# Causal attention layer: exponentials in pieces of 1024 columns, the exponential table loaded again behind each root, and the layers of the last four tiles in batches of two, one and one

## The chip, the core and the metric

The kernel runs on one core of one Trainium2 chip. The metric is the time of one execution on the device in microseconds; a change of 0.2% is 4 us here. The core has a matrix engine (TensorE; PE in the profile, PEld its weight loads), a vector engine (VectorE, DVE), a scalar engine for functions such as the exponential and the root (ScalarE, ACT), a general engine (GpSimd, POOL), and queues that start transfers (SyncE, SP). Each engine works through its own list of instructions; semaphores order them against each other. TensorE writes its results into a small accumulator memory (PSUM) from which the other engines copy them into the working memory (SBUF).

## What is computed

The input is an image of 256 channels and 64 x 64 positions. A first layer (windowed linear attention, not touched by the change) adds to it. Then the 4096 positions become tokens of 256 numbers, and a causal attention layer with a small network follows; a routed network of two experts ends the kernel. Cut to what matters here:

```python
t = _to_tokens(x)                                   # 4096 tokens x 256
t = t + _L1_attn_ref(_ln_t(t), ...)
t = t + _L1_ffn_ref(_ln_t(t), ...)

def _L1_attn_ref(x, ...):
    q, k, v = x @ Wq.T + bq, x @ Wk.T + bk, x @ Wv.T + bv
    A = where(causal, q @ k.T, MASK_FILL) / sqrt(256)
    A = softmax(A)
    out = _layernorm(A @ v + x, g_ln, beta_ln)
    h = relu(out @ W1.T + b1) @ W2.T + b2
    return _layernorm(h, g_lnff, beta_lnff)
```

The router of the last layer takes the mean over all tokens, so no expert work can start before the causal layer is through with its last token.

## The kernel before

The causal layer (`causal_attention`, L891) works on 32 tiles of 128 tokens, all in float32. Four tiles make a group `g`. The tiles 31 down to 12 are "large" and drive the outer loop, round by round; the tiles 0 to 11 are "small", and each of the first twelve rounds takes one of them along. From round 12 on, in which tile 19 is attended, there is no small tile left.

Four functions do the work:

- `queries(g)` (L911): two groups of matmuls make the queries `qT` of four tiles; ScalarE copies them out (L918). `need` calls it once for each group.
- `scores(i)` (L939): in parts of 512 columns, PE multiplies queries by keys into the accumulator `pa` (L957), of which there are two; ScalarE copies each part into the row buffer `s` or `ss` (L959), POOL masks the diagonal, VectorE takes the maximum of each part (L965). After the last part the maxima are merged into `nb` (L968, L969) and one exponential runs over the whole row, up to 4128 columns (L970).
- `attend(i)` (L974) returns steps. Step by step PE transposes four blocks of exponentials into `pt` (L987; two buffers), VectorE copies them to `sT` (L990), and PE multiplies them with the values into `po` (L1001). The last step ends with `finish`: division, addition of the input, statistics, and the tile is noted in `done`.
- `layers(g, j0, j1)` (L1031) returns the six stages that follow the attention for the tiles j0 to j1 of a group: `first` (root of the variances, normalisation, L1041), `turn` (transposes L1049, copies `aT` L1050), `hidden` (matmuls L1058, Relu L1060), `last` (matmuls L1068, addition L1070, statistics, root, L1075 and L1076, statistics), `norm` (root, normalisation L1083; nothing for PE), `turn_again` (transposes L1091, ScalarE's copies L1092 that also sum for the router).

Three stages contain a root. `rsqrt` (L708) takes it on ScalarE (Sqrt, L709) and inverts it on VectorE (L710). ScalarE holds one table of functions at a time; where the next function needs another one, the build puts a table load ahead of it (ACT_TABLE_LOAD in the trace).

The order on PE is the order in which the program is written (`tc.manual_schedule(engines={PE})`); the build's planner chooses the order of the other engines' instructions. The stages of `layers` are put into a list `later`, and each call of `one()` takes the next stage from it. In each round the order is: scores of the small tile and `one()`; all parts but the last of the next large tile's scores, `one()`, the first transposes of this round's large tile, the last part; half of its steps, `one()`, the other half; the small tile's attention; `one()`. In the last round alone every step is followed by `one()`. Thus some 17 us lie between `last` and `turn_again` of a group in most rounds.

The last group (tiles 12 to 15, `BIG` is 12) is batched in its own way: when three of its tiles are through (15, 14, 13) their layers start together, and tile 12's layers come alone at the very end. `given.parts` counts the batches, and `sums` has a column for each.

The opening: while the first row (tile 31) is scored in eight parts, the values are computed in between. Then round 0 begins with `need(0)`, the queries of the small tiles 0 to 3.

Of the kernel before, what the change touches and what calls it, by code (L numbers as in the profile page):

```python
# [11 lines left out]
F32 = mybir.dt.float32  # L12
BF16 = mybir.dt.bfloat16
I32 = mybir.dt.int32
AF = mybir.ActivationFunctionType
# [4 lines left out]
P = 128  # L20
# [684 lines left out]
    nc.vector.bn_aggr(out=mv, in_=st)  # L705


def rsqrt(nc, var, eps):  # L708
    nc.scalar.activation(var, var, AF.Sqrt, bias=eps)  # L709
    nc.vector.reciprocal(var, var)  # L710


BIG = NT - 20
# [146 lines left out]
class Given:  # L860
# [3 lines left out]
    def __init__(self, nc, a, pool, causal):  # L864
        def tile(name, shape, src=None):
            s = pool.tile(shape, F32, name=name)
            if src is not None:
                nc.gpsimd.dma_start(out=s, in_=src)
            return s

        self.gam, self.bet = causal.row["gamma"], causal.row["beta"]
        self.b1 = tile("b1", [NE, FF], a["b1"])
        self.b2 = tile("b2", [NE, D], a["b2"])
        self.wr = tile("wr", [P, DC, NE], a["Wr"].rearrange("(p c) e -> p c e", c=DC))
        self.br = tile("br", [P, NE], a["br"].partition_broadcast(P))
        self.ei = tile("ei", [P, NE])
        nc.gpsimd.iota(self.ei, pattern=[[1, NE]], base=0, channel_multiplier=0, allow_small_or_imprecise_dtypes=True)
        self.pi = tile("pi", [P, 1])
        nc.gpsimd.iota(self.pi, pattern=[[0, 1]], base=0, channel_multiplier=1, allow_small_or_imprecise_dtypes=True)

        self.before = tile("before", [P, NE, NE])
        nc.gpsimd.memset(self.before, 1.0)
        nc.gpsimd.affine_select(out=self.before, in_=self.before, compare_op=ALU.is_gt, fill=0.0, base=0,
                                pattern=[[1, NE], [-1, NE]], channel_multiplier=0)
        self.after = tile("after", [NT, D + 1])
        self.stats = tile("stats2", [P, NT, 2])
        self.sums = tile("sums2", [P, DC, NQ + 1])
        self.parts = 0


def causal_attention(tc, t, ident, eps5, causal, big, given):  # L891
# [4 lines left out]
    with ExitStack() as ctx:  # L896
# [42 lines left out]
        def scores(i):  # L939

            n = (i + 1) * P
            large = i >= BIG
            s = sm.tile([P, N + NT if large else BIG * P + NT], F32, name="s" if large else "ss")
            ss[i] = s
            g, starts = i // 4, list(reversed(range(0, n, 512)))
            nbs = sm.tile([P, 10], F32, name="nbs")

            nc.gpsimd.memset(s[:, n : n + NT], -3e38)  # L948
            if i < NT - 1:
                nc.gpsimd.memset(s[:, n + i : n + i + 1], MASK_FILL)  # L950

            def part(at):
                b = starts[at]
                m = min(512, n - b)
                pp = ps.tile([P, 512], F32, name="pa")
                for c in range(DC):
                    nc.tensor.matmul(pp[:, 0:m], lhsT=qTs[g][:, c, i * P - g * 512 : n - g * 512],  # L957
                                     rhs=x[b // 512][c][:, 0:m], start=(c == 0), stop=(c == DC - 1))
                nc.scalar.activation(s[:, b : b + m], pp[:, 0:m], AF.Identity, bias=v[i][:, D + 1 : D + 2])  # L959
                if at == 0:  # L960
                    diag = s[:, i * P : n]
                    nc.gpsimd.affine_select(out=diag, in_=diag, compare_op=ALU.is_ge, fill=MASK_FILL,
                                            base=0, pattern=[[-1, P]], channel_multiplier=1)
                    m += NT
                nc.vector.tensor_reduce(nbs[:, at : at + 1], s[:, b : b + m], AX.X, ALU.max)  # L965
                if at == len(starts) - 1:
                    nb = sm.tile([P, 1], F32, name="nb")
                    nc.vector.tensor_reduce(nb, nbs[:, 0 : len(starts)], AX.X, ALU.max)  # L968
                    nc.vector.tensor_scalar_mul(nb, nb, -1.0 / 16.0)  # L969
                    nc.scalar.activation(s[:, 0 : n + NT], s[:, 0 : n + NT], AF.Exp, bias=nb, scale=1.0 / 16.0)  # L970

            return [lambda at=at: part(at) for at in range(len(starts))]

        def attend(i):  # L974

            n = (i + 1) * P
            s = ss[i]
            cols = [(j * P, P) for j in range(i + 1)] + [(n, NT)]
            groups = [cols[at : at + 4] for at in range(0, len(cols), 4)]
            g = i // 4  # L980
            state = {}

            def turn(at):
                pt = ps.tile([P, 512], F32, name="pt")
                sT = sm.tile([P, 512], F32, name="sT", bufs=3)
                for j, (b, m) in enumerate(groups[at]):
                    nc.tensor.transpose(pt[0:m, j * P : (j + 1) * P], s[:, b : b + m], ident)  # L987
                full = P * sum(m == P for _, m in groups[at])
                if full:
                    nc.vector.tensor_copy(sT[:, 0:full], pt[:, 0:full])  # L990
                if full < P * len(groups[at]):
                    nc.vector.tensor_copy(sT[0:NT, full : full + P], pt[0:NT, full : full + P])
                state[at] = sT

            def add(at):
                if at == 0:
                    state["acc"] = ps.tile([P, 512], F32, name="po")
                acc, sT = state["acc"][:, 0 : D + 1], state.pop(at)
                for j, (b, m) in enumerate(groups[at]):
                    rhs = v[b // P][:, 0 : D + 1] if m == P else after  # L1000
                    nc.tensor.matmul(acc, lhsT=sT[0:m, j * P : (j + 1) * P], rhs=rhs, start=(b == 0), stop=(m != P))  # L1001
                if at == len(groups) - 1:
                    finish(acc)

            def finish(acc):
                if g not in atts:
                    atts[g] = (sm.tile([P, 4, D], F32, name="att", bufs=3), sm.tile([P, 4, 2], F32, name="mvs", bufs=3), [])
                att, mvs, done = atts[g]
                xn = normalised(nc, sm, t[:, i, :], stats[:, i, 0:1], stats[:, i, 1:2], "xn", 2)
                l = sm.tile([P, 1], F32, name="l")  # L1010
                nc.vector.reciprocal(l, acc[:, 0:1])
                aj = att[:, i - 4 * g, :]
                nc.vector.scalar_tensor_tensor(aj, acc[:, 1:], l, xn, op0=ALU.mult, op1=ALU.add)
                statistics(nc, sm, aj, mvs[:, i - 4 * g, :])
                done.append(i)
                if 4 * g != BIG:
                    if len(done) == 4:
                        later.extend(layers(g, 0, 4))
                elif len(done) == 3:
                    later.extend(layers(g, 1, 4))  # L1020
                elif len(done) == 4:
                    later.extend(layers(g, 0, 1))

            def step(at):
                if at + 1 < len(groups):
                    turn(at + 1)
                add(at)

            return [lambda: turn(0)] + [lambda at=at: step(at) for at in range(len(groups))]

        def layers(g, j0, j1):  # L1031
# [3 lines left out]
            state = {}  # L1035

            def first():
                rsqrt(nc, mvs[:, j0:j1, 1], eps5)
                for j in js:
                    aj = att[:, j, :]  # L1040
                    nc.vector.tensor_scalar(aj, aj, mvs[:, j, 0:1], mvs[:, j, 1:2], op0=ALU.subtract, op1=ALU.mult)  # L1041
                    nc.gpsimd.tensor_add(t[:, 4 * g + j, :], t[:, 4 * g + j, :], row["beta_lnff"])
# [19 lines left out]
            def last():  # L1062
                y, hT = att, state["hT"]
                mvy = sm.tile([P, 4, 2], F32, name="mvy")
                for j in js:
# [3 lines left out]
                                         start=(c == 0), stop=(c == DC - 1))  # L1069
                    nc.vector.tensor_add(y[:, j, :], py[:, 0:D], row["b2"])  # L1070
                    statistics(nc, sm, y[:, j, :], mvy[:, j, :])
                rsqrt(nc, mvy[:, j0:j1, 1], eps5)
                for j in js:
                    yj, tj = y[:, j, :], t[:, 4 * g + j, :]
                    nc.vector.scalar_tensor_tensor(yj, yj, mvy[:, j, 0:1], row["g_lnff"], op0=ALU.subtract, op1=ALU.mult)  # L1075
# [1 line left out]
                    statistics(nc, sm, tj, given.stats[:, 4 * g + j, :])  # L1077

            def norm():
                rsqrt(nc, given.stats[:, 4 * g + j0 : 4 * g + j1, 1], eps5)  # L1080
                for j in js:
                    s = given.stats[:, 4 * g + j, :]
                    nc.vector.tensor_scalar(att[:, j, :].rearrange("p (c q) -> p c q", c=DC),  # L1083
# [15 lines left out]
        with tc.manual_schedule(engines={mybir.EngineType.PE}):  # L1099
# [16 lines left out]
            for at, part in enumerate(scores(larges[0])):  # L1116
                part()
                if at < 3:
                    causal.values(6 - at, value_psum)
                if at == 4:  # L1120
                    behind()
            for r, i in enumerate(larges):
                small = smalls.pop(0) if smalls else None
                if small is not None:
# [5 lines left out]
                if r + 1 < len(larges):  # L1130
# [4 lines left out]
                    one()  # L1135
                    todo.pop(0)()
                    parts[-1]()
                if r == len(larges) - 1:
                    while todo:
                        todo.pop(0)()  # L1140
                        one()
# [189 lines left out]
```

## Time and profile before

| | us |
|---|---|
| median of 3 runs | 1993.42 (1993.35 to 1994.79) |
| the profiled execution, its own time | 1994.53 |
| its span, first to last instruction | 1992.8 |
| window layer, until the causal stage (about) | 0 to 1018 |
| first causal matmuls to the end of tile 20's round | 1018 to 1552 |
| rounds of tiles 19 to 13 | 1552.25 to 1713.5 |
| tile 12 and the last layers | 1713.5 to 1748.5 |
| router | 1748.5 to 1762 |
| experts | 1762 to 1993 |

The stages of the causal layer by window: in the rounds of tiles 19 to 13 PE is busy 152.19 of 161.25 us at full clock, DVE 87.47 and ACT 57.75. In the 35 us from 1713.5 to 1748.5 PE is busy 24.32 us, and the mean granted clock is 0.78. There are 32 exponentials of scores with 12 table loads ahead of them (L970), each load 1283 ns.

How to read the lines below: in the page's first part, busy time, share of the span and number of instructions; in the chain, shares of the span by engine. A line of waits has who waited for whom, the total in us, how often, and the longest. A line of the timeline has the start, the duration, the engine, the line of the kernel, the operation, what it writes and reads with shapes, the number of instructions merged, and in brackets the idle time of the engine before it and what ended it.

### The profile page before, as it was taken

How to read it: one execution, taken by the hardware profiler on the slowest of the kernel's cores; microseconds unless marked ns; L12 is line 12 of the kernel's file. 1: busy time of each engine (PE TensorE's matmuls, PEld its weight loads, DVE VectorE, ACT ScalarE, POOL GpSimd, SP SyncE). 2: the span in 40 equal slices, each digit the busy share in tenths (PEclk: the TensorE clock that was granted, in tenths of full speed). 3: DMA queues.
4: the chain of work that ended last, by engine and by line, in shares of the span. 5: the costliest groups of instructions: out<-in, count | busy, mean ns of one | idle time of the engine just before them, and what ended most of it. 6: DMA issues, size and time to landing. Idle time of an engine off the chain costs nothing.

```text
span 1992.8 us, 46271 instructions
## 1 busy us (share of the span) xinstructions
PE 1859.6 (93%) x20326; PEld 1218.4 (61%) x20326; DVE 1000.5 (50%) x2190; ACT 777.4 (39%) x1331; POOL 431.8 (22%) x709
## 2 busy tenths in 40 slices
PE   4999999999999999999999999999999999879998
PEld 2655565555665555555575656665666666657777
DVE  4644555544554565555663444554553655443343
ACT  1566444444456644444414233233333234223322
POOL 1384323232155123333110000000000000031220
PEclk9999999999999999999999999999999999879999
DMA  7211100000331100000100000000000000010000
GB/s 242 82 52 45 29 13 18 13 18 12 104 92 40 45 18 18 13 13 13 50 2 0 1 0 1 0 1 0 1 0 1 0 1 0 1 43 22 21 22 22
DMA packets 66890, 53.34 MB, mean 27 GB/s; under 512 B 37568, under 2 KB 56792, under 8 KB 66688
## 3 DMA queue, kind: packets, MB, share of 16 engines
q1 hardware_dynamic: 57296, 31.87, 5.8%
q10 hardware_dynamic: 8128, 14.67, 2.1%
q0 software_dynamic: 1264, 3.84, 0.6%
q8 instruction: 159, 2.61, 0.6%
q14 instruction: 43, 0.35, 0.1%
HBM read 32.93 MB, written 17.44 MB: 25 GB/s over the span
## 4 chain that ended last, share of the span: by engine, by line
PE 42%; DVE 6%; ACT 3%; issue 1%; POOL 0%; ACTq 0%; DVEq 0%; POOLq 0%
PE po L1001 11%; PE pa L957 10%; PE ph L1265 6%; PE py L1285 6%; PE pt L987 2%; PE pm L1058 1%; PE acc L391 1%; PE pm L1068 1%; DVE lnst L704 1%; PE ps L505 1%; DVE sT L990 1%; PE ps L358 1%; DVE nbs L965 1%; PE pm L916 1%; ACT s L970 1%
## 5 line engine op out<-in xcount | busy, mean ns | idle before, releaser
L327 ACT ACTIVATE pm<-ps 128x512 f32<-128x512 f32 (+19 forms) x734 | 362.4, 558 | 348.4 <-issue 194.1
L329 DVE TENSOR_SCALAR pm<-ps 128x512 f32<-128x512 f32 (+23 forms) x442 | 267.6, 636 | 315.7 <-PE ps L358 234.5
L391 PE MATMUL acc<-pm,vh 128*32 128x248 f32 (+22 forms) x3424 | 218.5, 356 | 16.8 <-DVE pm L329 16.7
L358 PE MATMUL ps<-q,kh 32*128 32x248 f32 (+23 forms) x3424 | 204.8, 354 | 0.0
L957 PE MATMUL pa<-k,qT 128*128 128x512 f32 (+3 forms) x416 | 180.2, 574 | 7.1 <-ACT qT L918 5.6
L349 PE MATMUL ps<-table,table 32*128 32x192 bf16 (+19 forms) x2512 | 143.1, 261 | 24.4 <-ACT rn L477 8.4
L990 DVE COPY sT<-pt 128x512 f32<-128x512 f32 (+3 forms) x144 | 92.7, 644 | 142.9 <-PE pt L987 142.7
L391 PEld LDWEIGHTS acc<-pm,vh 128*32 128x32 f32 x3424 | 87.3, 110 | 108.5 <-issue 60.8
L349 PEld LDWEIGHTS <-table 32*128 32x128 bf16 x2512 | 50.0, 92 | 162.5 <-issue 155.7
L358 PEld LDWEIGHTS ps<-q,kh 32*128 32x128 f32 x3424 | 142.6, 188 | 7.3 <-issue 2.5
L426 POOL TENSOR_TENSOR y<-y,rn 128x512 f32<-128x512 f32 x32 | 41.3, 1290 | 449.5 <-DVE y L425 297.9
L959 ACT ACTIVATE s<-pa,v 128x512 f32<-128x512 f32 (+3 forms) x112 | 73.8, 661 | 152.1 <-PE pa L957 151.9
L957 PEld LDWEIGHTS pa<-k,qT 128*128 128x128 f32 x416 | 75.7, 191 | 89.3 <-issue 72.4
L965 DVE TENSOR_REDUCE nbs<-s 128x1 f32<-128x512 f32 (+4 forms) x120 | 77.6, 652 | 80.4 <-ACT s L959 59.1
L1285 PE MATMUL py<-w,hT 128*128 128x256 f32 x512 | 111.8, 379 | 0.0
L1001 PE MATMUL po<-kh,sT 128*128 128x257 f32 x406 | 102.8, 395 | 8.7 <-DVE sT L990 8.5
L1285 PEld LDWEIGHTS py<-w,hT 128*128 128x128 f32 x512 | 97.3, 190 | 15.7 <-issue 1.9
L391 PE MATMUL acc<-pm,v 128*32 128x192 f32 (+11 forms) x1600 | 98.5, 360 | 3.9 <-DVE pm L329 2.4
L358 PE MATMUL ps<-q,k 32*128 32x192 f32 (+11 forms) x1600 | 98.4, 359 | 0.0
L1001 PEld LDWEIGHTS po<-kh,sT 128*128 128x128 f32 x406 | 74.7, 195 | 22.4 <-DVE sT L990 13.2
L505 PE MATMUL ps<-l0wo,y 128*128 128x256 f32 x384 | 87.0, 383 | 0.0
L948 POOL MEMSET s<- 128x32 f32 x20 | 2.5, 124 | 376.4 <-PE pt L987 348.4
(304 smaller groups left out, 2899.0 us busy)
## 6 DMA issues: line engine op xcount, KB each, us to landing
oscratch<-ov ACTq DMA_DIRECT2D x32, 256.0 KB
ov<-oscratch SPq DMA_DIRECT2D x32, 256.0 KB
t<-in_xT SPq DMA_DIRECT2D x32, 128.0 KB
vscratch<-v SPq DMA_DIRECT2D x32, 128.0 KB
vh<-vscratch SPq DMA_DIRECT2D x16, 256.0 KB
raw<-in_x SPq DMA_DIRECT2D x7, 512.0 KB
raw<-in_x ACTq DMA_DIRECT2D x7, 512.0 KB
out<-y SPq DMA_DIRECT2D x7, 512.0 KB
```

The costliest lines, as they stand in the source:

```text
L327: nc.scalar.activation(dst, src, AF.Relu)
L329: nc.vector.tensor_scalar_max(dst, src, 0.0)
L349: nc.tensor.matmul(got[h][:, spot].rearrange("p (y x) -> p y x", y=part.r1 - part.r0), lhsT=spread[hs, int(part.vertical), :], rhs=bias[hs ...
L358: nc.tensor.matmul(got[h][:, spot].rearrange("p (y x) -> p y x", y=part.r1 - part.r0), lhsT=keys[hs], rhs=q[hs, part.r0 : part.r1, part.c0 ...
L391: nc.tensor.matmul(out, lhsT=v, rhs=pm[:, h, spot].rearrange("p (y x) -> p y x", y=part.r1 - part.r0), start=fresh, stop=(left[key] == 0), ...
L505: nc.tensor.matmul(pt[:, i * D : (i + 1) * D], lhsT=ys[wi, Y][:, (2 * j + i) * P : (2 * j + i + 1) * P], rhs=wo[:, n, :], start=(n == 0), ...
L957: nc.tensor.matmul(pp[:, 0:m], lhsT=qTs[g][:, c, i * P - g * 512 : n - g * 512], rhs=x[b // 512][c][:, 0:m], start=(c == 0), stop=(c == DC ...
L965: nc.vector.tensor_reduce(nbs[:, at : at + 1], s[:, b : b + m], AX.X, ALU.max)
L990: nc.vector.tensor_copy(sT[:, 0:full], pt[:, 0:full])
L1001: nc.tensor.matmul(acc, lhsT=sT[0:m, j * P : (j + 1) * P], rhs=rhs, start=(b == 0), stop=(m != P))
L1265: nc.tensor.matmul(ph, lhsT=w1v[:, e, c, f, :], rhs=x2[g][c], start=(c == 0), stop=(c == DC - 1))
L1285: nc.tensor.matmul(py, lhsT=hT[:, e, f, j * P : (j + 1) * P], rhs=w2v[:, e, f, :], start=(e + f == 0), stop=(e == 1 and f == FC - 1))
```

## The change

- `rsqrt` gets an optional pool. With it, the root goes into a tile of its own (`root`), an exponential of one column with scale 0 follows on ScalarE, whose result nobody reads, and the inversion reads `root`. The three roots in `layers` use it; the experts' and the first norm's don't.
- The exponential of a row is cut at each multiple of 1024 columns; the last piece takes the 32 columns behind the row along.
- The last group's layers start when two of its tiles are through (15 and 14), then for tile 13 alone, then for tile 12 alone; `sums` has one more column.
- `need(smalls[0])`, the queries of tiles 0 to 3, is called behind part 5 of the first row's scores; the call at the start of round 0 then finds them.
- The loop in which every step is followed by `one()` runs in all rounds without a small tile, the rounds of tiles 19 to 12, not in the last round alone. After the loop no steps are left, and the two further calls of `one()` of the round follow at once.

```diff
-def rsqrt(nc, var, eps):
-    nc.scalar.activation(var, var, AF.Sqrt, bias=eps)
-    nc.vector.reciprocal(var, var)
+def rsqrt(nc, var, eps, pool=None):
+
+    if pool is None:
+        nc.scalar.activation(var, var, AF.Sqrt, bias=eps)
+        nc.vector.reciprocal(var, var)
+        return
+    n = var.shape[-1]
+    root = pool.tile([P, 4], F32, name="root", bufs=3)
+    nc.scalar.activation(root[:, 0:n], var, AF.Sqrt, bias=eps)
+    nc.scalar.activation(pool.tile([P, 1], F32, name="unread"), root[:, 0:1], AF.Exp, scale=0.0)
+    nc.vector.reciprocal(var, root[:, 0:n])
...
-        self.sums = tile("sums2", [P, DC, NQ + 1])
+        self.sums = tile("sums2", [P, DC, NQ + 2])
...
-                    nc.scalar.activation(s[:, 0 : n + NT], s[:, 0 : n + NT], AF.Exp, bias=nb, scale=1.0 / 16.0)
+                    ends = list(range(1024, n, 1024)) + [n + NT]
+                    for b, e in zip([0] + ends, ends):
+                        nc.scalar.activation(s[:, b:e], s[:, b:e], AF.Exp, bias=nb, scale=1.0 / 16.0)
...
-                elif len(done) == 3:
-                    later.extend(layers(g, 1, 4))
-                elif len(done) == 4:
-                    later.extend(layers(g, 0, 1))
+                elif len(done) > 1:
+                    later.extend(layers(g, 4 - len(done), 4 if len(done) == 2 else 5 - len(done)))
...
-                rsqrt(nc, mvs[:, j0:j1, 1], eps5)
+                rsqrt(nc, mvs[:, j0:j1, 1], eps5, sm)
...
-                rsqrt(nc, mvy[:, j0:j1, 1], eps5)
+                rsqrt(nc, mvy[:, j0:j1, 1], eps5, sm)
...
-                rsqrt(nc, given.stats[:, 4 * g + j0 : 4 * g + j1, 1], eps5)
+                rsqrt(nc, given.stats[:, 4 * g + j0 : 4 * g + j1, 1], eps5, sm)
...
                 if at == 4:
                     behind()
+                if at == 5:
+                    need(smalls[0])
...
-                if r == len(larges) - 1:
+                if small is None:
                     while todo:
                         todo.pop(0)()
                         one()
```

## The prediction, made before the changed kernel was built or run

> **What bounds the kernel now.** I read the page first (busy shares, chain), then the list of waits of the TensorE for the causal stage (1009 to 1765 us), then the timeline at the places that list points to, last the stage windows for the granted clock.
>
> ```profile
> PE 1859.6 (93%) x20326; PEld 1218.4 (61%) x20326; DVE 1000.5 (50%) x2190; ACT 777.4 (39%) x1331; POOL 431.8 (22%) x709
> PE 42%; DVE 6%; ACT 3%; issue 1%; POOL 0%; ACTq 0%; DVEq 0%; POOLq 0%
> ```
>
> PE is the bound; the others matter where PE, which runs in the order written by hand, stops for them. The waits of PE in the causal stage:
>
> ```profile
> PE pt L1091 <- DVE att L1083: 7.5, 2, 4.0
> PE pa L957 <- ACT qT L918: 6.7, 6, 4.1
> PE pt L987 <- ACT kh L1092: 3.8, 2, 2.1
> PE pa L957 <- ACT s L959: 1.3, 3, 0.6
> ```
>
> All PE waits there are under 50 us, so the change has little to win and the order of PE has much to lose. The largest single wait that ScalarE causes is at the opening:
>
> ```profile
> 1065.91 1.28 ACT L970 ACT_TABLE_LOAD   x1 [1.20 <-DVE nb L969]
> 1067.20 3.73 ACT L970 ACTIVATE s<-s,nb 128x4128 f32<-128x4128 f32 x1
> 1070.85 1.25 ACT L918 ACTIVATE qT<-pm,ik 128x512 f32<-128x512 f32 x2
> 1071.57 1.37 PE L957 MATMUL pa<-k,qT 128*128 128x128 f32 x4 [4.15 <-ACT qT L918]
> ```
>
> The queries of group 0 sit behind the exponential of tile 31; PE stands 4.15 us. The window 1070.6 to 1077.5 then has a granted clock of 0.51, about 3 us more.
>
> The layers behind the attention are a DVE chain. Here `last` of tiles 16 to 19 starts on PE, and `norm` can write the first normalised tile 12.06 us later:
>
> ```profile
> 1675.83 3.83 PE L1068 MATMUL pm<-ik,hT 128*128 128x256 f32 x16
> ...
> 1682.34 0.30 ACT L709 ACTIVATE mvy<-mvy,eps 128x4 f32<-128x4 f32 x1
> ...
> 1686.78 0.30 ACT L709 ACTIVATE stats<-stats,eps 128x4 f32<-128x4 f32 x1
> ...
> 1687.89 1.38 DVE L1083 TENSOR_SCALAR att<-t,stats 128x256 f32<-128x256 f32 x4
> ```
>
> In that window DVE is busy nearly throughout (11.71 of 12.2 us); 1.76 are three maxima, 0.58 an sT copy, 1.6 the end of a tile's attention. The chain alone is thus some 9.3 us to the first and 10.7 to the last of four tiles. Today PE has a half attend and a whole set of scores to do in it.
>
> [...] The trace has 1.28 for each load but the ACTIVATE right behind it (1065.91 to 1067.20), so I take 1.29 for a switch; 0.43 us at 160 columns and 3.73 at 4128 give 0.294 + 0.833 per 1000 elements[...]. [...] the pieces help only where the build places other work between them.
>
> **The change part by part.**
>
> *Pieces.* One exponential becomes up to four. Tiles 12 to 15 get one more piece, 16 to 23 two, 24 to 31 three, the small 8 to 11 one: 4 + 16 + 24 + 4 = 48 pieces, each 0.294 − 0.09 = 0.2 us: 10 us of ACT. It lies beside attend steps, in which ACT has little to do: 0 on the path. Where something is queued behind, it comes up to 0.6 us later.
>
> *Queries of group 0 earlier* (after part 5). The same 8 matmuls (3.43 us) move ahead of the last two parts, so the exponential of tile 31 starts 3.4 us later, its load at about 1069.3 (1.28), four pieces until 1075. PE, now free of qT, does the small part (0.43), tile 30's first two parts (1.29 + 1.72) until 1070.7, and needs the first of the two `pa` buffers again; its eviction is queued behind the pieces: 1075 + 0.58 − 1070.7 = 4.8 us in place of 4.15. If an eviction goes in behind the first piece (1071.7), the wait is 1.6 and the clock stays up: −2.5 − 3. Bounds −5.5 and +0.7. The evictions are written after the exponential and all pieces are ready at once, so I take +0.5.
>
> *Table back behind each root.* Every root in the stage now costs a load, 0.30, a second load, and about 0.2 for the unread exponential: 3.07 us of ACT instead of 1.58; the exponential of scores saves its 1.28. Roots among score evictions: 1317.85, 1322.29 and the pair near 1486 and 1490.6. PE writes a part each 1.72 us into two buffers, so 1.5 us more on ACT become about 1.25 each: 4 × 1.25 = +5.0. At 1218.94 and 1385.79 qT waits behind the load: +0.8 and +0.5. Gone: the small exponentials' loads that held evictions (1.4) and two waits for v L1092 (0.7). Sum +4.2; bounds 0 (the build puts roots in idle stretches) and +9 (6 pairs at the full 1.5).
>
> *Layers after every step from tile 19 on.* This is the big part. `if small is None` holds in the last eight rounds, not one. A step is 4 transposes and 8 matmuls, 2.18 us (1562.51 to 1564.69); `norm` has nothing for PE.
> - Tile 19: turn of tiles 20 to 23, step, hidden, step, last, step, norm, step, turn_again. Between the start of `last` and turn_again PE has 3.66 + 2 × 2.18 = 8.0 us; DVE needs 9.3 + 1.5 for the copies, and 1.4 until the fourth tile. 3.5 lost, 0.5 for the evictions, 1.0 for the clock. Then turn, hidden and last of tiles 8 to 11 stand one behind the other: 1.05 for aT (copy 0.81 behind the tile's own end), 0.45 for the Relu. 6.5.
> - Tile 18: norm, one step, turn_again: PE has about 13.8, DVE as much; 0.5, and 1.5 for its evictions behind the exponential. 2.0.
> - Tile 16: it ends, and first, turn, hidden follow with nothing between. From the last matmul to the first att tile 2.6 us (today 1713.6 to 1716.4, with part of an sT copy between), four tiles 3.6, transposes, aT 0.81: hidden at 4.65, of which PE works 0.9. 3.75, clock 2.0: 5.75.
> - Tile 15: last, turn(0), part, step, norm, step, turn_again: PE 10.2; DVE 9.3 + 1.3 + 1.9 = 12.5 and the last tile's lag: 2.8.
> - Tile 14: the new batch of two (14, 15), again first, turn, hidden in a row: 3.1, clock 1.0: 4.1.
> - Tile 13: turn_again of the two: 0.5. Its own first, turn, hidden stall as they do today at 1716.58.
>
> Sum 21.7 (clock 4.0 of it, bounds 0 and 11[...]). Today's waits from 1552 to 1698 that go with the old places: kh 3.8, sT 1.9, v 0.8, aT 1.6: −8.1. Net +13.6.
>
> *The end.* Today tile 13 ends at 1713.5 and tile 12's closing chain starts at 1734.69: 21.2 us with layers of three tiles woven in. With one tile: 3.2 until hidden, 0.9, 0.43, 1.1 for last, four steps 7.4, turn_again and its wait 1.2, clock 2.5: 16.8. Then the chain of tile 12 saves 1.8 of queueing but pays a root load between its mvy and stats roots (idle there is 1.57, two loads and 0.2 are 2.8: +1.2) and 0.3 before its evictions: −0.3. Together −4.7; bounds −8 and 0.
>
> Sum: 0.5 + 4.2 + 13.6 − 4.7 = +13.6 on the profiled execution's own 1994.53 (its span is 1992.8). The median shown is 1993.42, 1.1 lower; the difference goes onto it: **2007.0**.
>
> **The rivals.**
> - *Heavier*: each added wait halves the clock for a full window (+7), and every table pair stops the evictions (+4.8), less some 2.5 where the two fall together: about 2016. For it: a mere 2.42 us did that at 1716. Against: the steps between keep PE busy.
> - *Lighter*: no clock drop (−4), roots in idle stretches (−4.2): 1998.8. For it: the planner runs the first roots early today (1554.33, for a group of the next round).
> - *No change*: lighter, and evictions between the pieces at the opening (−6.0): 1992.8.
> - *Faster*: ScalarE serves between pieces everywhere. Opening −5.5, all its waits of rounds before tile 19 (qT 2.2, s 1.3, v 0.7) −4.2, and in the layers no clock drop and no eviction or Relu behind an exponential, 21.7 − 4.0 − 2.0 = 15.7, less 8.1: +7.6; the end −4.7. Sum −6.8: 1986.6. It decides if the layers' net is under about 10. Against it: what PE waits for in the layers is DVE arithmetic, which no ScalarE order shortens.
> - That the table does not come back (one set with both functions) is excluded: the trace loads for each of the two.
>
> **Chances.** Forecast 0.50, heavier 0.12, lighter 0.12, no change 0.10, faster 0.16. A change of 0.2% is 4 us, about what a measurement here can tell. Slower 0.74, same 0.10, faster 0.16. Range 1993 to 2016 leaves out the faster case and part of the heavier; the likeliest case's own range is 2001 to 2014.
>
> **What would show it.** Around 60 table loads in the causal stage instead of some 24; a wait of PE for att L1083 of 3 us or more while tile 19 is attended, and for att L1041 at the ends of tiles 16 and 14; the 4.15 us wait for qT gone but one of like size for `s` L959 a few us later; a shorter stretch from tile 13's end to the router. If PE has no wait over 2 us between tiles 19 and 14, the layer term is wrong, and with it the sign.

## The result, and the profile after

The changed kernel takes 2009.38 us (median of 5 runs, 2007.19 to 2021.9) beside 1994.79 for the kernel before on the same chip: a ratio of 1.0089, with a 95% interval of 1.007 to 1.0108. It is slower by 14.6 us in the medians and by some 18 by the ratio (14 to 21.5 by its interval). The forecast was 2007.0. The profiled execution took 2008.99 us with a span of 2007.3, which is 14.5 us more than the profiled execution before.

The line of the page of the changed kernel that matters: busy time, share of the span and number of instructions of each engine.

```profile
PE 1861.3 (93%) x20334; PEld 1221.2 (61%) x20334; DVE 1002.4 (50%) x2195; ACT 831.9 (41%) x1448; POOL 434.4 (22%) x709
```

ScalarE (ACT) is busy 54.5 us longer, with 117 instructions more, and still has over half of its time free. TensorE's busy time is the same but for 1.7 us. So the loss of 14.5 us is not work on any engine; it is PE standing still or running slowly. The waits of PE in the causal stage of the changed kernel (who waits for whom, total us, times, longest):

```profile
PE pt L1099 <- DVE att L1091: 13.7, 5, 5.3
PE pt L1057 <- DVE att L1049: 10.5, 4, 2.7
...
PE pa L965 <- ACT s L967: 4.7, 2, 4.4
PE pt L997 <- ACT k L1100: 3.0, 2, 2.3
PE pa L965 <- ACT qT L926: 2.3, 4, 0.9
```

The wait for the normalised tiles `att` ahead of `turn_again` (now L1099) has grown from 7.5 us in two to 13.7 in five. The wait ahead of `turn` (L1057) is 10.5 in four; in the kernel before it had been a single one:

```profile
PE pt L1049 <- DVE att L1041: 2.4, 1, 2.4
```

The wait for queries has shrunk from 6.7 to 2.3, but one for a score eviction has come up to 4.7.

That last exchange is the opening. The same place as before, in the timeline of the changed kernel:

```profile
1068.99 1.28 ACT L980 ACT_TABLE_LOAD   x1 [1.05 <-DVE nb L977]
1070.28 4.29 ACT L980 ACTIVATE s<-s,nb 128x1024 f32<-128x1024 f32 x4
1074.48 0.42 ACT L980 ACTIVATE ss<-ss,nb 128x160 f32<-128x160 f32 x1
1074.80 1.14 ACT L967 ACTIVATE s<-pa,v 128x384 f32<-128x384 f32 x2
1075.42 2.08 PE L965 MATMUL pa<-kh,qT 128*128 128x512 f32 x2 [4.41 <-ACT s L967]
```

The four pieces run without a gap and the evictions come behind them: cutting the exponential did not let anything in between. PE stands 4.41 us where it had stood 4.15.

And the chain behind `last`, where the first large loss lies. In the round of tile 19, in the timeline of the changed kernel:

```profile
1567.21 3.62 PE L1076 MATMUL pm<-ik,hT 128*128 128x256 f32 x16
...
1573.37 0.30 ACT L716 ACTIVATE root<-mvy,eps 128x4 f32<-128x4 f32 x1 [6.15 <-DVE mvy L705]
...
1577.95 0.30 ACT L716 ACTIVATE root<-stats,eps 128x4 f32<-128x4 f32 x1 [1.46 <-DVE stats L705]
...
1578.49 1.38 DVE L1091 TENSOR_SCALAR att<-t,stats 128x256 f32<-128x256 f32 x4
...
1579.05 2.21 PE L1099 MATMUL pt<-ident,att 128*128 128x128 f32 x8 [3.87 <-DVE att L1091]
```

From the start of `last` to the first transpose of `turn_again` are 11.84 us. In the kernel before, 17.1 us lay between the two for the same group, filled with other work of PE, and it did not wait for `att` (no bracket behind the second line):

```profile
1577.21 3.83 PE L1068 MATMUL pm<-ik,hT 128*128 128x256 f32 x16
...
1594.34 1.04 PE L1091 MATMUL pt<-ident,att 128*128 128x128 f32 x8
```

Now it has 8 us of work there.

Around these waits the granted clock was 0.58 to 0.72. Windows around the opening and four of the new waits in the changed kernel (window, length, busy us of each engine with instructions, granted clock, DMA share, GB/s):

```profile
1072.00:1080.00 8.00, 4.58 (x6) 2.00 (x7) 1.22 (x3) 4.62 (x7) 0.29 (x1) 0.60 0.01 2
1578.00:1584.00 6.00, 4.95 (x19) 3.57 (x19) 3.31 (x11) 3.39 (x9) 0.23 (x2) 0.72 0.00 0
1655.00:1661.00 6.00, 4.77 (x12) 2.35 (x13) 3.09 (x7) 1.65 (x3) 0.47 (x1) 0.72 0.00 0
1680.00:1687.00 7.00, 5.04 (x17) 3.85 (x18) 2.13 (x6) 4.63 (x8) 0.00 (x0) 0.58 0.00 0
1707.00:1716.00 9.00, 7.09 (x19) 5.13 (x20) 2.80 (x9) 3.10 (x6) 0.93 (x2) 0.62 0.01 2
```

The last four of these clocks stand in a stretch that had run at a clock of 1.00 before (1552 to 1713 us).

Taking the same points of PE's list in both traces gives the account. Each row is the difference (after minus before) that arises in that stretch:

| stretch of PE's list | us |
|---|---|
| up to the first causal scores | −0.5 |
| from there to the end of tile 31 (the opening) | +0.4 |
| to the end of tile 20 | −3.0 |
| rounds of tiles 19 to 14 | +9.7 |
| from the end of tile 14 to that of tile 13 | +14.1 |
| from there to the experts' first matmul | −5.0 |
| the experts | −1.2 |
| span | +14.5 |

The rounds that the loop now covers cost 23.8 us, the early rounds gain 3.0, and the end gains 5.0. The opening costs 0.4, and the first and the last but one row (−0.5 and −1.2) lie in code that the change does not touch.

### The profile page after: what moved, and what is told of

It reads as the page before. It is cut to its first block, busy times and chain, and to the rows that moved or that the text cites. A ratio compares the mean times of both kernels' runs of the same rounds, so it can differ in the third digit from the quotient of the medians.

```text
span 2007.3 us, 46414 instructions
## 1 busy us (share of the span) xinstructions
PE 1861.3 (93%) x20334; PEld 1221.2 (61%) x20334; DVE 1002.4 (50%) x2195; ACT 831.9 (41%) x1448; POOL 434.4 (22%) x709
## 4 chain that ended last, share of the span: by engine, by line
PE 44%; DVE 6%; ACT 2%; issue 1%; POOL 0%; DVEq 0%; ACTq 0%; POOLq 0%
PE po L1011 12%; PE pa L965 11%; PE ph L1275 6%; PE py L1295 6%; PE pt L997 2%; PE pm L1066 2%; PE acc L391 1%; DVE lnst L704 1%; PE ps L358 1%; PE pm L924 1%; PE ps L505 1%; DVE sT L1000 1%; PE pm L1076 1%; DVE t L1084 1%; DVE nbs L973 1%
## 5 line engine op out<-in xcount | busy, mean ns | idle before, releaser
L1011 PEld LDWEIGHTS po<-kh,sT 128*128 128x128 f32 x406 | 73.5, 192 | 19.0 <-DVE sT L1000 10.4
```

## The experiments

Each kernel ran beside the kernel before on the same chip; medians are compared with the median of before there (1994.06, 1993.58 or 1994.6 us). My theory was that the order on PE, the loop, costs all of it. The rival was that the table pairs do, with the pieces.

**The loop taken back.** The changed kernel with one line as it was:

```diff
-                if small is None:
+                if r == len(larges) - 1:
```

> The changed kernel with the loop 'every step followed by a stage' back in the last round alone; table, pieces, early queries and batches of two, one, one kept. Theory 1 (the order on PE costs the time: stages follow so closely that PE waits for VectorE's chain): the 14.6 us go, and the 3 us that the rounds before tile 19 gained stay: 1990 to 1994, a ratio to before of 0.997 to 1.000. Theory 2 (the second table load behind each root holds ScalarE): most of the loss stays, 2003 or more.

Measured: 1994.19 us (13 runs) against 1994.06, ratio 1.0003 (0.9993 to 1.0014). All of the loss goes with the loop, and everything else of the change, without the loop, adds up to nothing. The ratio is just outside the expected 0.997 to 1.000: the 3 us that the early rounds had gained do not remain as a net gain.

**The loop alone.** The kernel before with the opposite edit.

> The kernel before with nothing changed but the loop (rounds of tiles 19 to 12). Theory 1: all of the loss and the 3 us that the table gave back on top: 2008 to 2013 against 1994.8, waits of PE for att L1083 of 3 us or more in tile 19's round. Theory 2: less than 5 us slower.

Measured: 2004.44 (6 runs), ratio 1.006 (1.0041 to 1.0078). The direction is right; the size, +10.4, is under what I had expected. Together with the other parts the loop costs 15 to 17 (the changed kernel less the one with the loop taken back), alone 10. The new batches may be some of that difference (see below); what makes up the rest was not shown.

**The table alone.** The kernel before with the new `rsqrt` and its three calls in `layers`:

```diff
-                rsqrt(nc, mvs[:, j0:j1, 1], eps5)
+                rsqrt(nc, mvs[:, j0:j1, 1], eps5, sm)
...
-                rsqrt(nc, mvy[:, j0:j1, 1], eps5)
+                rsqrt(nc, mvy[:, j0:j1, 1], eps5, sm)
...
-                rsqrt(nc, given.stats[:, 4 * g + j0 : 4 * g + j1, 1], eps5)
+                rsqrt(nc, given.stats[:, 4 * g + j0 : 4 * g + j1, 1], eps5, sm)
```

> The kernel before with the exponential table loaded again behind each root of the layers, nothing else. The prediction's term: 4 us slower. From the trace after: the rounds before tile 19 get about 3.4 us shorter, the end of the last tile about 1.5 longer: 1991 to 1994, ratio 0.998 to 1.000. Theory 2: 8 us slower or more.

Measured: 1991.9 (14 runs), ratio 0.9985 (0.9976 to 0.9995): the second load does not cost, it gains. The timeline of ScalarE in this kernel at one of the roots among score evictions shows why:

```profile
1316.51 1.28 ACT L716 ACT_TABLE_LOAD   x1
1317.81 0.30 ACT L716 ACTIVATE root<-mvy,eps 128x4 f32<-128x4 f32 x1
1318.01 0.67 ACT L967 ACTIVATE s<-pa,v 128x512 f32<-128x512 f32 x1
1318.70 1.28 ACT L717 ACT_TABLE_LOAD   x1
1319.99 0.20 ACT L717 ACTIVATE unread<-root 128x1 f32<-128x1 f32 x1
1320.10 0.67 ACT L967 ACTIVATE s<-pa,v 128x512 f32<-128x512 f32 x1
```

The planner put an eviction between the root and the unread exponential. PE writes a part each 1.72 us into two buffers, and no single load of 1.28 us stopped it here: PE has no gap over 0.1 us between 1314 and 1321 us. In exchange, the loads ahead of the small tiles' exponentials are gone, and with them the waits of PE for a score eviction that the kernel before had (1.3 us). Relative to the first causal scores this kernel is 6.4 us ahead when tile 12 ends. Of that, up to 1.7 is clock and not table: the kernel before has 17.1 us at half clock in this stretch, this execution 13.7. Then it loses 2.8 us in two places. PE's wait ahead of the `turn_again` of tiles 15 to 13 is 4.84 us in place of 3.45, as VectorE inverts the root before it only behind tile 12's division, 1.9 us after the root and not 0.4. The wait ahead of the last `turn_again` is 5.29 in place of 4.04: in the closing chain of tile 12 the second load stands between two roots and nothing covers it.

**The table everywhere but in the last group.** The same three calls, each with `None if tail else sm` in place of `sm`; `tail` holds for the last group. One of the three, against the kernel before:

```diff
-                rsqrt(nc, mvs[:, j0:j1, 1], eps5)
+                rsqrt(nc, mvs[:, j0:j1, 1], eps5, None if tail else sm)
```

> The kernel before with the table loaded back behind the roots of all groups but the last (tiles 12 to 15). The table alone shortened the causal stage by 6.3 us until tile 12 ends and lengthened the closing chain by 2.8. If that chain pays for the root's own load between two roots: 1988 to 1989.5, ratio 0.997 to 0.998. If not, as the table alone: 1991 to 1992.

Measured: 1986.58 (9 runs), ratio 0.9965 (0.9951 to 0.9978). It gains 5 us more than the table everywhere, somewhat more than reckoned.

**The pieces alone.** The kernel before with the exponential cut at each 1024 columns.

> The kernel before with the exponentials in pieces of 1024 columns, nothing else. Theory 1: 48 pieces more at 0.2 us each lie beside PE's work, 0 to +1 us, ratio 0.9995 to 1.001; PE's wait for qT at the opening stays (4.15 us and 0.6). Rival (ScalarE takes other work between pieces): that wait falls under 2 us and the kernel gains 3 to 7 us.

Measured: 1996.42 (14 runs), ratio 1.0019 (1.0009 to 1.0029). Both expectations miss, mine by a little: the cut costs 2.4 us in the medians, 2 to 6 by the interval. ScalarE's busy time grows by 8.9 us for 48 pieces, 0.19 each, as reckoned; but what stands queued behind an exponential comes later by that, and at one such place the clock fell in the profiled execution. In the timeline of this kernel in the round of tile 18:

```profile
1593.87 2.61 ACT L972 ACTIVATE s<-s,nb 128x1024 f32<-128x1024 f32 x3
1596.39 0.57 ACT L1094 ACTIVATE kh<-pt 128x512 f32<-128x512 f32 x1
1597.11 0.72 PE L989 MATMUL pt<-ident,s 128*128 128x128 f32 x4 [2.48 <-ACT kh L1094]
```

PE's wait there was 2.13 us before, at full clock; now it is 2.48, and the six matmuls of 128x257 that start at 1597.62 take 2.78 us, where six that start at 1591.75, ahead of it, take 1.57: by that pace a halved clock (waits beside which it fell, and others beside which it did not, are in the last section).

**The queries of tiles 0 to 3 moved, alone.** The kernel before with `need(smalls[0])` behind part 5.

> The kernel before with the queries of tiles 0 to 3 moved behind part 5 of the first row, nothing else. My theory (the copies leave the queue behind the exponential of tile 31, but the next score evictions take their place behind it): PE's wait of 4.2 us for qT becomes one of 3.5 to 5 us for an eviction of scores a few us later, with the same halved clock after it; -1 to +1 us against the kernel before. Rival (the wait goes, as the move is made for): 4 to 7 us faster. Nothing of the computation is left out.

Measured: 1995.05 (14 runs), ratio 1.0007 (0.9996 to 1.0017): nothing. The profile has the wait that moved:

```profile
1070.87 3.74 ACT L970 ACTIVATE s<-s,nb 128x4128 f32<-128x4128 f32 x1
1074.51 0.41 ACT L970 ACTIVATE ss<-ss,nb 128x160 f32<-128x160 f32 x1
1074.83 1.14 ACT L959 ACTIVATE s<-pa,v 128x384 f32<-128x384 f32 x2
1075.45 1.12 PE L957 MATMUL pa<-kh,qT 128*128 128x512 f32 x2 [3.87 <-ACT s L959]
```

The half clock that was expected behind this wait did not come in this execution (the granted clock is 1.00 from 1072 to 1080 us), which is the fastest of the 14 (1990.58 us). Whether it came in the others is not on record.

**The order in which the opening is written.** The move, and the pieces of tile 31 alone, each written behind one part of tile 30's scores in place of one behind the other:

```diff
-                    nc.scalar.activation(s[:, 0 : n + NT], s[:, 0 : n + NT], AF.Exp, bias=nb, scale=1.0 / 16.0)
+                    if i == NT - 1:
+                        ends = list(range(1024, n, 1024)) + [n + NT]
+                        for b, e in zip([0] + ends, ends):
+                            held.append(lambda b=b, e=e: nc.scalar.activation(
+                                s[:, b:e], s[:, b:e], AF.Exp, bias=nb, scale=1.0 / 16.0))
+                    else:
+                        nc.scalar.activation(s[:, 0 : n + NT], s[:, 0 : n + NT], AF.Exp, bias=nb, scale=1.0 / 16.0)
...
                     for part in parts[:-1]:
                         part()
+                        if held:
+                            held.pop(0)()
```

> The kernel before with the queries of tiles 0 to 3 behind part 5, and the exponential of tile 31 alone in four pieces, each written behind one of the first four parts of tile 30's scores, so that evictions stand ahead of pieces in ScalarE's queue. If the wait at the opening (4.15 us before, 4.41 after) is a matter of the order in that queue: no wait over 1.5 us there, no halved clock at 1070 to 1080, 5 to 7 us less: 1987 to 1989, ratio 0.9965 to 0.9975. If the two accumulators set it whatever the order: 0 to -1 us.

Measured: 1986.79 (6 runs), ratio 0.996 (0.9943 to 0.9976), as expected if the order in the queue is what counts. The timeline of this kernel at the opening:

```profile
1074.79 1.15 ACT L973 ACTIVATE s<-s,nb 128x1024 f32<-128x1024 f32 x1
1075.84 0.41 ACT L976 ACTIVATE ss<-ss,nb 128x160 f32<-128x160 f32 x1
1076.16 1.14 ACT L959 ACTIVATE s<-pa,v 128x384 f32<-128x384 f32 x2
1076.77 0.70 PE L957 MATMUL pa<-kh,qT 128*128 128x512 f32 x1 [1.26 <-ACT s L959]
```

One piece only stands ahead of the eviction, and PE waits 1.26 us, without a halved clock (the matmul behind the wait takes 0.70 us, the two in the changed kernel 2.08). The move alone and the pieces alone had gained nothing. So here the pieces helped by the work that waits being written between them, and not by being short.

**Empty slots between the stages.** The changed kernel, with stages that do nothing put between `norm` and `turn_again` of the last three full groups, so that more steps lie between:

```diff
+            wait = [lambda: None]
+            if g in (2, 4, 5):
+                return [first] + 2 * wait * (g == 4) + [turn, hidden, last, norm] + 3 * wait + [turn_again]
             return [first, turn, hidden, last, norm, turn_again]
```

> The changed kernel, its loop kept, with empty places in the list of stages of groups 5, 2 and 4: three between norm and turn_again, two between first and turn of group 4. The same work, a stage less often. If the loss is VectorE's chain with too few PE steps in it: the waits for att L1091 (3.87, 2.24) and att L1049 at the end of tile 16 (2.72) fall under 1.5 us each, and with the halved clock behind them 9 to 13 us go: 1997 to 2000. If stages between single steps cost by themselves: 2006 or more.

Measured: 2012.74 (5 runs), ratio 1.0092 (1.0077 to 1.0108): a plain miss. PE's waits for `att` in these rounds, in the changed kernel:

```profile
PE pt L1099 <- DVE att L1091: 6.1, 2, 3.9
PE pt L1057 <- DVE att L1049: 5.4, 2, 2.7
```

And in this kernel:

```profile
PE pt L1099 <- DVE att L1091: 10.4, 4, 4.1
PE pt L1057 <- DVE att L1049: 2.7, 1, 2.7
```

The wait ahead of `turn` at the end of tile 16 is gone, but ahead of `turn_again` one of 3.09 us came for tiles 8 to 11, and that in tile 15's round grew from 2.24 to 4.10. (The fourth, of 0.70, is in the changed kernel too, just behind the stretch of its list.) The two calls of `one()` at the end of a round follow one another with no PE work between them, so an empty slot there moves a stage on without giving the chain any time; and at a tile's end VectorE has `finish` to do as well, ahead of `norm`. From `last` to `turn_again` it is 12 to 14 us in three of the places. This left two explanations: that the slots were no time, or that stages after every step cost by themselves.

**The stages held until behind the scores.** The changed kernel with its loop, but in the rounds of tiles 19 to 14 `turn_again` waits in the list until the call behind the next tile's scores, and `turn` too where `first` came at a round's end:

```diff
+            held = []
+
             def one():
-                if later:
+                if later and later[0].__name__ not in held:
                     later.pop(0)()
...
                 if small is None:
+                    held[:] = ["turn_again"] if r < len(larges) - 2 else []
                     while todo:
                         todo.pop(0)()
                         one()
+                    if r < len(larges) - 2:
+                        held[:] = ["turn", "turn_again"]
...
                 one()
+                held.clear()
```

> The changed kernel with its loop, but in the rounds of tiles 19 to 14 turn_again is held until the place behind the next large tile's scores, and turn too where first came at the end of a round, so that 14 us or more of PE work lie between last and turn_again and a set of scores between first and turn. My theory (the loop costs because the chain from last to turn_again takes 12 to 14 us wherever its stages are put, and PE is given less work than that inside it): PE's waits for att in the rounds of tiles 19 to 14 (3.87, 2.72, 2.24, 2.71 us and the evictions behind them) fall under 0.7 us each, with the halved clock that follows them, 8 to 12 us come back: 1997 to 2001 us. Rival (a stage after every step costs by itself, since its VectorE and ScalarE work delays the sT copies and evictions of the steps around it, so the place of turn_again matters little): 2005 us or more, with waits of PE for sT and for evictions in place of those for att. Nothing of the computation is left out.

Measured: 1994.6 (21 runs) against 1994.6, ratio 1.0 (0.999 to 1.001). It gives back nearly all of the loop's cost, more than reckoned, although the loop still runs. The waits of PE in this kernel from 1552 to 1722 us:

```profile
PE pt L1099 <- DVE att L1091: 6.8, 3, 3.4
PE pt L997 <- DVE aT L1058: 1.9, 4, 0.5
PE pt L997 <- ACT kh L1100: 1.8, 2, 1.5
PE po L1011 <- DVE sT L1002: 1.0, 1, 1.0
```

The waits ahead of `turn` (L1057) are gone from these rounds. At the held places `turn_again` still waits 1.92 and 1.43 us, not under 0.7 as I had written: with the scores in between the chain itself took 13.3 and 14.2 us there. The 3.4 is tile 13's round, where nothing is held. Holding the two stages decides it; the other stages after every step cost little by themselves.

**The batches as before, with the loop.** The changed kernel, its last group as three tiles and then one (and one column less in `sums`):

```diff
-                elif len(done) > 1:
-                    later.extend(layers(g, 4 - len(done), 4 if len(done) == 2 else 5 - len(done)))
+                elif len(done) == 3:
+                    later.extend(layers(g, 1, 4))
+                elif len(done) == 4:
+                    later.extend(layers(g, 0, 1))
```

> The changed kernel with the batches of the last group as before (tiles 15, 14, 13 together, then tile 12) in place of two, one and one. My theory: with the loop in all the last rounds the two, one and one costs more than it brings: a second chain stands in front of PE at the end of tile 14 (waits 2.71, 0.70, 2.33 us with two half-clock windows of 3.4 to 6.8 us), against some 5 us that the end is shorter, of which 4.4 are PE work only moved: this kernel is 3 to 6 us faster than the changed one, 2003 to 2006.5 us. Rival (as the prediction had it, the batches bring 4.7 us at the end and cost 4.6 in the rounds, about nothing net): 2008 to 2010 us. If it is over 2012 us, the batches are worth their place. Nothing of the computation is left out.

Measured: 2007.2 (6 runs), ratio 1.0063 (1.0046 to 1.008), between the two expectations. The interval overlaps that of the changed kernel (1.007 to 1.0108), and in the profiles the two reach the experts within 0.8 us of each other, counted from the first causal scores. What the batches are worth with the loop, a loss of 2 us by the medians or 5 by the ratios, is not clear of noise and stays open.

**The two that gained, together.** The opening in the order written above, and the table everywhere but in the last group, on the kernel before.

> The two of these together (table back behind the roots of all groups but the last; pieces of tile 31 between evictions, early queries), the loop and the batches as before. If they add: 1981 to 1984, ratio 0.9935 to 0.995. If they share a cause: 1986 or more.

Measured: 1983.85 (6 runs), ratio 0.9947 (0.9932 to 0.9963). This lies where it was expected, but the two gains measured apart, 6.8 and 7.0 us, make 13.8, and together they are 9.7. They add up in the main; whether the missing 4 us are noise or something that the two share is not shown (the intervals allow either). This version beats both kernels: by some 10 us the one before, by some 25 the changed one, reckoned through the kernel before.

## Why the prediction was right, and where its sum was wrong

The forecast was 2007.0, the direction was right and the time is within 2.4 us. The mechanism that carried the forecast, the loop, is shown by taking it back, by doing it alone and by holding two of its stages. The sum, +13.6, came near +14.5 with two wrong terms in it that cancel: that it came so near is luck.

| term | predicted | in the profile after | a part alone |
|---|---|---|---|
| opening | +0.5 | +0.4 | +0.5 (the move) |
| pieces | 0 | not separable | +2.4 |
| table, rounds before tile 19 | +4.2 | −3.0 | −2.2 (whole kernel) |
| layers, rounds of tiles 19 to 15 | +8.95 | +9.7 to the end of tile 14 | |
| layers, tile 14's end and tile 13 | +4.6 | +14.1 | |
| the end | −4.7 | −5.0 | |

*Opening.* Right, with its reason. The wait for queries became one for an eviction of like size, and only another written order takes it away.

*Pieces.* Right for attend steps, which cover them, but not for what is queued behind: the prediction said "up to 0.6 us later" and then counted 0. Alone they cost 2.4 us; in the profiled execution a halved clock at one of these places is part of it.

*Table.* The step that failed is "1.5 us more on ACT become about 1.25 each: 4 × 1.25". It takes the second load as one block with the first. The planner placed the eviction that was due between the two, and each load alone, 1.28 us where PE takes 1.72 for a part, left PE without a gap over 0.1 us at the place shown. What was left of the term is its gain: the small tiles' loads that went. The lower bound given, 0, did not hold either, as it did not subtract these. At tile 12's closing chain the prediction's +1.2 for the load between two roots came: PE's last wait is 5.29 us, with the table alone and in the changed kernel, in place of 4.04.

*Layers, tiles 19 to 15* (6.5 + 2.0 + 5.75 + 2.8 − 8.1 in the prediction). The expected waits are there: 3.5 us ahead of `turn_again` in tile 19's round, 3.87 measured; at the end of tile 16 3.75 for `turn` and `hidden` together, 2.72 measured ahead of `turn`; in tile 15's round 2.8, measured 2.24 and then 1.31 for the eviction. The sum is right to 0.8 us, but not each round: in tile 15's, 6.8 us at half clock follow, by my estimate about 2.8 us more (half of PE's 5.52 us busy in them) that the prediction put at nothing, while the waits in tile 18's round, put at 2.0, were 0.64.

*Layers, tile 14's end and tile 13* (4.1 + 0.5). This is the term that was mis-sized, by 9.5 us. About 4.4 us of it is PE's own work on the layers of tiles 14 and 15: the end's term counted it as leaving, since "with one tile" the stretch is shorter, and the layers' term never counted it as arriving. Of the rest, about 2.4 us are the clock at the end of tile 14 (6.8 us at a clock of 0.50 cost up to half of that, 3.4, by my estimate; 1.0 was counted) and about 2.5 the waits at `turn_again`. At the end of tile 14 and in front of `turn_again` (timeline of the changed kernel):

```profile
1708.15 0.73 DVE L1049 TENSOR_SCALAR att<-att,mvs 128x256 f32<-128x256 f32 x2
1708.70 1.14 PE L1057 MATMUL pt<-ident,att 128*128 128x128 f32 x4 [2.71 <-DVE att L1049]
...
1726.83 1.28 ACT L980 ACT_TABLE_LOAD   x1 [0.57 <-DVE stats L718]
1727.42 0.78 PE L1099 MATMUL pt<-ident,att 128*128 128x128 f32 x4 [0.70 <-DVE att L1091]
1728.13 1.89 ACT L980 ACTIVATE s<-s,nb 128x1024 f32<-128x1024 f32 x2
1730.02 0.36 ACT L1100 ACTIVATE k<-pt 128x256 f32<-128x256 f32 x1
1730.53 0.55 PE L997 MATMUL pt<-ident,s 128*128 128x128 f32 x3 [2.33 <-ACT k L1100]
```

"turn_again of the two: 0.5" is 0.70 and then 2.33 us, as the exponential of tile 12 came with its load between the root and the unread exponential, ahead of the evictions. The wait of 2.71 us, close to the 3.1 reckoned, is followed by 6.8 us at half clock, with PE busy 7.09 of 9 us.

*The end.* Right in size, but as the mirror of that omission: 4.4 of its 5.0 us is the PE work that has moved.

The signs named beforehand came: 55 table loads in the causal stage (about 60 said, 24 before; each takes 1283 ns, and in both traces one stands at each switch between root and exponential and none elsewhere), the wait of over 3 us in tile 19's round, those at the ends of tiles 16 and 14, a wait for `s` in place of that for queries, and a stretch from tile 13's end to the router that is 5 us shorter. Of the rivals, the faster one fell with the opening: ScalarE serves nothing between the pieces. The lighter one came nearer on the table (nothing, in place of +4.2) and was wrong on the clock.

The two errors, −7.2 on the table and +10.3 on the layers, largely cancel. Had the table's sign been right and nothing else, the forecast would have been near 2000, outside its own case's range of 2001 to 2014.

## What to carry to other kernels

Where an engine runs in a fixed order, a stage may follow another only when the work placed between them is as long as the chain that the other engines have to run in that time (here 12 to 14 us from `last` to `turn_again`); count it in microseconds of work, not in slots of the schedule. Cutting a long instruction into pieces gives its queue nothing unless the work that waits is written between the pieces (here 2.4 us lost with the pieces alone, 6.8 gained with the evictions written between them, the queries moved too). A second table load cost PE nothing here where an eviction stood between it and the first, and 1.3 us where a root followed a root on the chain that ended last. When a sum takes work out of one stretch, it must put it into another, or the two terms must be worked out as one.

## What the runs showed of the hardware

The clock fell beside some waits and not beside others. A wait of 2.13 us (the kernel before, at 1597.51) left it at 1.00. Waits of 2.24 (the changed kernel, at 1680.65) and 2.42 (the kernel before, at 1716.58) each stand beside 6.83 us at a clock of 0.50, and one of 2.48 (the pieces alone, at 1597.11) beside matmuls at that pace, while 2.33 and 2.52 (the changed kernel, at 1730.53 and 1736.83) left it at 1.00. So did the 3.87 us wait at the opening of the kernel with the queries moved (1.00 from 1072 to 1080 us). The prediction's terms for the clock were its author's estimates. For the rounds of tiles 19 to 14 they sum to 4.0 us; the changed kernel has four stretches at 0.50 there, from 1578.76, 1657.27, 1681.16 and 1708.47 us, of 3.41, 3.41, 6.83 and 6.83 us. By my estimate they cost up to 10.2 us, half of their sum.

In these traces the length of a wait alone does not tell what follows it. In the profiled executions of the kernel before and of the changed one the granted clock changes 25 times each, between 1.00 and 0.50 alone, and within each the times of the changes lie multiples of 3.41 us apart. Cut at such points into steps of 3.41 us, the wait of 2.13 is 0.90 in one step and 1.23 in the next, and the clock stays at 1.00. The wait of 2.24 lies whole in one step, and the clock is 0.50 in the next. The wait of 3.87, cut in two at 1073.54, is 1.96 and 1.91, at a clock of 1.00 in both. Windows of 3.41 us, first the kernel with the queries moved, then the changed kernel (the columns as above; the first busy time is PE's, the number of two decimals behind POOL's count the clock):

```profile
1070.13:1073.54 3.41, 1.45 (x4) 0.38 (x2) 0.00 (x0) 3.40 (x2) 0.00 (x0) 1.00 0.00 0
1073.54:1076.95 3.41, 1.50 (x4) 0.79 (x5) 1.16 (x2) 2.43 (x4) 0.29 (x1) 1.00 0.03 5
```

```profile
1677.75:1681.16 3.41, 1.17 (x6) 0.50 (x4) 3.34 (x13) 1.41 (x2) 0.00 (x0) 1.00 0.00 0
1681.16:1684.57 3.41, 2.10 (x9) 1.51 (x9) 0.31 (x1) 3.40 (x8) 0.00 (x0) 0.50 0.00 0
```

In the causal stage of the kernel before and of the changed one there were 8 steps at full clock in which PE stood for 2.12 to 3.41 us in all (by the trace, in which the ends of matmuls are modelled), and a half clock followed each. Of the 11 steps with 1.23 to 1.71 us it followed 3, and of those with 1.14 us or less none. Two waits added up in one of the 3: 0.96 and 0.76 us, at 1258 to 1261 us in the kernel before, 1.47 of it in one step, were followed by 3.41 us at 0.50. Why some of the 11 were followed by it and others not, and whether these counts hold for other kernels, was not shown. For a wait of 2 to 4 us I would count a chance of 1.7 to 3.4 us on top of it; that is an estimate, half of the 3.41 or 6.83 us at 0.50 that stand beside such waits here.
